# Moving the v projection of each second half into the first half's window, in a fused transformer block on one core

## The chip, the cores and the metric

The kernel runs on one core of a Trainium2 chip. The metric is the device time of one execution in microseconds (us), median of several runs. The engines are named as the profile names them: PE (TensorE matmuls), PEld (TensorE weight loads), DVE (VectorE), ACT (ScalarE), POOL (GpSimd) and SP (the queue that issues nearly all DMAs).

## What is computed

A transformer block with conditioned layer norms (D = 512 features, H = 16 heads of 32, hidden size 2048) over x of 8 sequences with 1024 tokens each, all in float32:

```python
mod = silu(condition) @ Wada + bada            # six vectors of 512 per sequence
sh_a, sc_a, gt_a, sh_m, sc_m, gt_m = split(mod, 6, axis=1)
xm = layernorm(x, g1, be1) * (1 + sc_a) + sh_a
q, k, v = heads(xm @ Wqkv)
x = x + gt_a * (softmax(causal(q @ k.T) * scale) @ v @ Wproj + bproj)
xm = layernorm(x, g2, be2) * (1 + sc_m) + sh_m
x = x + gt_m * (gelu(xm @ W1 + b1) @ W2 + b2)
```

## The kernel before

**Blocks and windows.** Each sequence is cut into two halves of 512 tokens, so there are 16 blocks n = 0 to 15; even n is a first half, odd n a second half. Through causality a first half attends to itself alone, a second half to both halves: it needs k and v of both. Window w is the stretch in which the attention of block w is issued. Beside it run the linear steps (projections and MLP) of neighbouring blocks, in an order written out by hand in a dictionary `plan[w]`, lines 236 to 269. Steps are `("k", n)`, `("q", n)`, `("v", n)` (projections of block n), `("proj", n)` (output projection), `("at", n)` and `("mt", n)` (transposes of the normalized rows, for attention and MLP), `("u", n, i)` (up projection, i = 0 to 3) and `("d", n, part)` (down projection, four parts). The MLP of block w - 1 begins in window w, and what is left over stands in `late` and opens window w + 1.

Before the change an odd window w opens with `late`, which holds ("u", w-2, 3), two parts of d, the transposes ("at", w+1), the other two parts of d; then comes ("v", w). An even window opens with two parts of d and ("v", w). Later in both come load_xr, proj (w-1), k (w+1), mt (w-1), q (w+1), and u of block w-1. Window 15 opens with one u, proj 14, mt 14 and four parts of d, then ("v", 15). Window 0 already holds ("v", 1); windows 0 and 1 are not touched.

**One projection** (`strassen`, line 773) is made with seven products of half size, each of four calls of `matmul`, and each of these four column-tiled TensorE instructions of 256 columns (line 205). The weights come as seven 256 KB pieces through a ring of nine tiles, loaded in the order of the plan by SP (`fetch`). Results leave the PSUM banks through DVE and ACT. Three PSUM banks (`ps_l`) serve all linear steps; four more form the one tile `st`/`sc` of the attention, one holds its output `po`.

**Attention.** A second half has 26 units of weights in its window, a first half 10. A unit is: scores `sc` (line 1476, row-tiled) and their maxima on DVE (line 1493) for the next group; then `weights_T`: `st` (lines 1557 and 1569, row-tiled), the exponential on ACT (line 1582), for diagonal units the mask on POOL (line 1587), sums of the weights on POOL (line 1695); then `weigh`: `po` (line 1610). TensorE works through one queue in the order in which the program was written; that order is chosen when the program is built, by a small model of each engine's clock. `step_aside` (line 1337) issues linear work ahead of an attention instruction until that instruction is ready by the model; `pace` adds to the linear work that is due, at a rate that spreads the linear work planned for a window over its attention:

```python
1720            stream["rate"] = planned_time(n) / mine * (0.7 if n == 0 else 1.0)
```

Where an attention step needs a result that is not made yet, the linear work is driven on until it is there, without any attention between. For v this stands in `close`, which issues the `po` of a unit:

```python
1333    def until(condition):
1334        while not condition():
1335            work()
1755        until(lambda: n - blocks[n][1] + parts[-1][0] // NTT in valued)
```

In a second half the first four units of a group use v of the first half, the others v of the second half; `valued` gets block n when its v is complete. `project_v` (line 882) may start once `free for v` of its block is set, which in the window of a first half happens at its first unit for both halves; `v` has two buffers. `("mt", n)` waits for `v done` of block n + 1 (line 1246), because it takes the buffer of the normalized input that v read.

The down projection (`down`, line 1073) subtracts halves of the hidden activations `hT` on DVE (line 1088) and through `either` (lines 162 and 165, which picks DVE or POOL by the model).

Of the kernel before, what the change touches and what calls it, by code (L numbers as in the profile page):

```python
# [22 lines left out]
def kernel(  # L23
# [66 lines left out]
    blocks = [(b, h) for b in range(B) for h in range(NHALF)]  # L90
# [140 lines left out]
    def mlp_steps(n):  # L231
        return [("u", n, i) for i in range(NQ)] + [("d", n, part) for part in range(4)]
# [8 lines left out]
    late = []  # L241
    for w in range(1, NB):
        n = w - 1
        m = mlp_steps(n)
        even = blocks[n][1] == 0
        rows_a = [("rows", blocks[n][0], "a")] if even else []
        rows_m = [("rows", blocks[n][0], "m")] if even else []
        own = m[:1] + ([("load_xa", w + 2)] if w + 2 < NB else []) + m[1:3]
        own += [("norm_a", w + 2)] if w + 2 < NB else []
        if w == NB - 1:  # L250
            steps = late[:1] + [("load_xr", n)] + rows_a + [("proj", n), ("mt", n)] + late[1:]
            steps += [("v", w)] + rows_m + own + m[3:6]
            late = m[6:]
        else:

            steps = late + [("v", w), ("load_xr", n)] + rows_a + [("proj", n), ("k", w + 1)]
            if w == 1:
                steps = [("load_xr", n)] + rows_a + [("k", w + 1), ("proj", n)]
            steps += [("mt", n), ("q", w + 1)] + rows_m + own
            at = [("at", w + 2)] if w + 2 < NB else []  # L260
            if blocks[w][1] == 0:

                late = m[3:6] + at + m[6:]
            else:
                steps += m[3:6] + at
                late = m[6:]
        plan[w] = steps
    n = NB - 1
# [1601 lines left out]
```

## Time and profile before

| what | value |
|---|---|
| median of 3 runs | 3526.36 us (3525.41 to 3528.59) |
| the profiled execution | 3526.6 us, span of its instructions 3524.9 us |
| granted TensorE clock, mean | 0.999 |
| DVE / ACT / POOL busy | 53% / 36% / 59% |
| LDWEIGHTS (PEld) busy | 51% |
| HBM traffic | 123 GB/s over the span |

The profile is one execution. Its busy time of an engine is the time in which at least one instruction of that engine ran; a wait's releaser is what ended the idle time. In the order of time, a row of the timeline is a run of equal instructions, with its start, its length and their count; in these rows a `matmul` call shows as eight PE records, so a projection is 224 of them.

### The profile page before, as it was taken

Reading aid. Unit: us, or ns where it says so; the run is one execution under the profiler, and the core shown is the slowest. Engines: PE = TensorE matmul, PEld = TensorE weight load, DVE = VectorE, ACT = ScalarE, POOL = GpSimd, SP = SyncE. Lnnn points to the kernel's source line nnn. Section 1 sums busy time; section 2 is a strip of 40 time slices with the busy share of each in tenths; the row PEclk is TensorE's granted clock in tenths of the full one; section 3 lists DMA queues with packets and bytes.
Section 4 is the critical chain, followed back from the end, with each engine's and each line's share of the span. In section 5 each row is a group of like instructions: output and inputs, shape, how many; then the busy total and the mean of one; then the engine's idle time right before and its main releaser. Section 6 shows DMA issues by size and latency. Waiting matters only on the chain.

```text
span 3524.9 us, 123741 instructions
## 1 busy us (share of the span) xinstructions
PE 3482.2 (99%) x56189; PEld 1800.1 (51%) x56189; DVE 1882.3 (53%) x2086; ACT 1286.5 (36%) x1422; POOL 2065.1 (59%) x2205
## 2 busy tenths in 40 slices
PE   7999999999999999999999999999999999999999
PEld 4444455445554554545545455454554545545445
DVE  5765664554635456364563645635446354554463
ACT  2335243352433514235152352514424244241521
POOL 3676755665456664576645766557664576644650
PEclk9999999999999999999999999999999999999999
DMA  6842334334343343533435334353343533434234
GB/s 208 267 143 89 115 109 120 123 106 142 107 139 103 109 142 103 155 100 100 145 99 159 97 103 139 101 157 99 104 139 100 156 101 108 131 100 151 89 118 137
DMA packets 319945, 441.76 MB, mean 125 GB/s; under 512 B 26569, under 2 KB 188677, under 8 KB 319421
## 3 DMA queue, kind: packets, MB, share of 16 engines
q1 hardware_dynamic: 319168, 433.54, 40.2%
q8 instruction: 443, 7.26, 0.8%
q14 instruction: 82, 0.66, 0.1%
q10 hardware_dynamic: 252, 0.29, 0.0%
HBM read 404.32 MB, written 29.41 MB: 123 GB/s over the span
## 4 chain that ended last, share of the span: by engine, by line
PE 93%; DVE 2%; POOL 2%; DMA 1%; issue 1%; ACT 1%; SPq 0%; DVEq 0%; POOLq 0%; ACTq 0%
PE bank L205 64%; PE sc L1476 9%; PE po L1610 7%; PE st L1569 7%; PE st L1557 2%; PE bank L656 2%; DVE mx L1493 2%; PE bank L1631 2%; POOL pT L1695 1%; PE bank L1531 0%; POOL hT L165 0%; DVE sc L1490 0%; DMA w<-in_L_cond_Wada_dram 0%; DMA hat<-in_x_dram 0%; DMA w<-in_L_cond_Wproj_dram 0%
## 5 line engine op out<-in xcount | busy, mean ns | idle before, releaser
L1695 POOL TENSOR_TENSOR pT<-pT,pT 128x256 f32<-128x256 f32 (+3 forms) x1254 | 1179.0, 975 | 202.0 <-ACT pT L1582 115.8
L1582 ACT ACTIVATE pT<-st 128x2048 f32<-128x2048 f32 x288 | 541.1, 1879 | 1046.0 <-PE st L1569 933.0
L205 PE MATMUL bank<-w,hT 128*32 128x256 f32 x14336 | 797.5, 379 | 0.1
L1493 DVE TENSOR_REDUCE mx<-sc 128x4 f32<-128x2048 f32 (+3 forms) x384 | 665.9, 1755 | 133.8 <-PE sc L1476 127.1
L205 PEld LDWEIGHTS bank<-w,hT 128*32 128x32 f32 x14336 | 451.9, 110 | 331.1 <-issue 26.6
L205 PE MATMUL bank<-xm_m,w 128*32 128x256 f32 x8192 | 499.4, 381 | 0.0
L205 PE MATMUL bank<-t_m,w 128*32 128x256 f32 x6144 | 383.9, 380 | 0.0
L205 PEld LDWEIGHTS bank<-xm_m,w 128*32 128x32 f32 x8192 | 252.1, 110 | 242.6 <-issue 80.9
L1587 POOL TENSOR_SCALAR_AFFINE_SELECT pT<-pT 128x512 f32<-128x512 f32 x256 | 165.2, 663 | 326.1 <-ACT pT L1582 324.6
L1476 PE MATMUL sc<-kT,qT 32*128 32x512 f32 (+3 forms) x3072 | 329.1, 520 | 5.7 <-DVE mx L1493 3.1
L1610 PE MATMUL po<-pT,v 128*32 128x512 f32 (+3 forms) x3072 | 305.6, 492 | 3.1 <-POOL pT L1587 3.1
L1490 DVE TENSOR_TENSOR sc<-sc,mask 128x1024 f32<-128x1024 f32 (+1 forms) x160 | 162.9, 1018 | 256.6 <-PE sc L1476 204.1
L1569 PE MATMUL st<-qT,kT 32*128 32x512 f32 (+3 forms) x3072 | 299.9, 486 | 0.0
L205 PEld LDWEIGHTS bank<-t_m,w 128*32 128x32 f32 x6144 | 192.1, 110 | 180.5 <-issue 52.7
L205 PE MATMUL bank<-xm_a,w 128*32 128x256 f32 x3968 | 250.3, 382 | 0.0
L197 DVE TENSOR_TENSOR hT<-bank,u_u 128x512 f32<-128x512 f32 x192 | 129.1, 686 | 158.1 <-PE bank L205 155.9
L165 POOL TENSOR_TENSOR qT<-top,rec 128x512 f32<-128x512 f32 x61 | 78.0, 1278 | 227.5 <-ACT rec L1649 227.5
L1476 PEld LDWEIGHTS sc<-kT,qT 32*128 32x128 f32 x3072 | 129.5, 183 | 155.1 <-ACT pT L1582 63.6
L205 PE MATMUL bank<-w,qT 128*32 128x256 f32 (+1 forms) x2944 | 191.0, 399 | 1.3 <-DMA w<-in_L_cond_Wproj_dram 1.3
L1030 ACT ACTIVATE hT<-hT,cols 128x512 f32<-128x512 f32 x256 | 164.2, 711 | 54.9 <-DVE hT L197 54.3
L205 PE MATMUL bank<-t_a,w 128*32 128x256 f32 x2944 | 183.9, 380 | 0.0
L205 PEld LDWEIGHTS bank<-xm_a,w 128*32 128x32 f32 x3968 | 122.9, 110 | 100.1 <-issue 17.6
(211 smaller groups left out, 3477.8 us busy)
## 6 DMA issues: line engine op xcount, KB each, us to landing
w<-in_L_cond_W_dram SPq DMA_DIRECT2D x384, 256.0 KB
w<-kept_up_S SPq DMA_DIRECT2D x256, 256.0 KB
w<-kept_down_S SPq DMA_DIRECT2D x256, 256.0 KB
w<-kept_qkv_S SPq DMA_DIRECT2D x180, 256.0 KB
w<-in_L_cond_Wqkv_dram SPq DMA_DIRECT2D x147, 256.0 KB
hat<-in_x_dram SPq DMA_DIRECT2D x64, 256.0 KB
xr<-in_x_dram SPq DMA_DIRECT2D x64, 256.0 KB
out_dram<-xr SPq DMA_DIRECT2D x64, 256.0 KB
```

The source lines that it names most:

```text
L165: nc.gpsimd.tensor_tensor(out, a, b, op)
L197: nc.vector.tensor_tensor(out, src, other, op)
L205: nc.tensor.matmul(ps[r, :], lhsT[:, r], rhs, start=start, stop=stop, skip_group_check=True)
L1030: nc.scalar.activation(hT[:, i, :], hT[:, i, :], AF.Gelu, bias=cols[:, O_B1 + f : O_B1 + f + 1])
L1476: nc.tensor.matmul(sc[:, j, c0 : c0 + w], qTs[n][r, gg, ts(qt, P)], keys_of(n, kh)[r, gg, :w], start=True, stop=True, skip_group_check=True,)
L1490: nc.vector.tensor_tensor(place, place, shape_of.to_broadcast(place.shape), ALU.add)
L1493: nc.vector.tensor_reduce(maxima[n, gg][:, kh, qt, :], sc[:, :, c0 : c0 + w], axis=AX.X, op=ALU.max)
L1569: nc.tensor.matmul(st[:, j, c0 : c0 + w], kT[r, gg, ts(k % NTT, P)], qT[r, gg, TB - w :], start=False, stop=True, skip_group_check=True,)
L1582: nc.scalar.activation(pT[:, :, :used], st[:, :, :used], AF.Exp, scale=scale)
L1587: nc.gpsimd.affine_select(diagonal, diagonal, pattern=[[0, HPG], [1, P]], compare_op=ALU.is_ge, fill=0.0, base=0, channel_multiplier=-1,)
L1610: nc.tensor.matmul(po[r, TB - w :], v[:, k % NTT, g * P + j * hd : g * P + (j + 1) * hd], pT[:, j, c0 : c0 + w], start=(k == 0), stop=last ...
L1695: nc.gpsimd.tensor_tensor(into, into, pT[:, j, c0 : c0 + w], ALU.add)
```

## The change

The v projection of block w, for odd w from 3 to 15, is taken out of window w (in windows 3 to 13 from behind `late`, in window 15 from behind the parts of d) and put into window w - 1, behind ("q", w) and ahead of the u steps that follow there. First halves keep theirs at the front of their own window. The guards, the buffers, the number of steps and the arithmetic are the same; the order in which SP loads the weight pieces follows the plan.

```diff
@@ -249,14 +249,14 @@
         if w == NB - 1:
             steps = late[:1] + [("load_xr", n)] + rows_a + [("proj", n), ("mt", n)] + late[1:]
-            steps += [("v", w)] + rows_m + own + m[3:6]
+            steps += rows_m + own + m[3:6]
             late = m[6:]
         else:
-            steps = late + [("v", w), ("load_xr", n)] + rows_a + [("proj", n), ("k", w + 1)]
+            steps = late + ([] if even else [("v", w)]) + [("load_xr", n)] + rows_a + [("proj", n), ("k", w + 1)]
             if w == 1:
                 steps = [("load_xr", n)] + rows_a + [("k", w + 1), ("proj", n)]
-            steps += [("mt", n), ("q", w + 1)] + rows_m + own
+            steps += [("mt", n), ("q", w + 1)] + ([("v", w + 1)] if blocks[w][1] == 0 else []) + rows_m + own
```

In this loop n is w - 1 and `even` is true when block n is a first half, that is, when w is odd.

## The prediction

> **What bounds the kernel now.** I read the page's busy times and chain first, then TensorE's busy time in three stretches (windows 0 and 1, windows 2 to 14, window 15 and the end), then its list of waits in the middle one.
>
> ```profile
> span 3524.9 us, 123741 instructions
> PE 3482.2 (99%) x56189; PEld 1800.1 (51%) x56189; DVE 1882.3 (53%) x2086; ACT 1286.5 (36%) x1422; POOL 2065.1 (59%) x2205
> PEclk9999999999999999999999999999999999999999
> PE 93%; DVE 2%; POOL 2%; DMA 1%; issue 1%; ACT 1%; SPq 0%; DVEq 0%; POOLq 0%; ACTq 0%
> ```
>
> ```profile
> 0.00:399.00 399.00, 372.18 (x6037) 1.00 0.52 166
> 399.00:3128.30 2729.30, 2724.08 (x43975) 1.00 0.40 120
> 3128.30:3525.00 396.70, 385.99 (x6188) 0.99 0.40 121
> ```
>
> ```profile
> engine line waited for: us in total, times, longest us
> PE bank L1531 <- POOL mcols L1515: 2.5, 4, 0.7
> PE sc L1476 <- DVE mx L1493: 1.6, 7, 0.5
> ```
>
> TensorE is never short of work. Six of the seven moves lie between 399 and 3128 us, and there it idles 2729.30 - 2724.08 = 5.2 us in all; its named waits there are 2.5 and 1.6 us. The other idle time is the start (399.00 - 372.18 = 26.8 us, before anything that changes) and window 15 with the end (396.70 - 385.99 = 10.7 us). The clock is granted in full. A move of work can thus take away only these few us, or add new idle time; what DVE, ACT and POOL gain or lose beneath costs nothing until TensorE waits.
>
> **What the move touches.** This is TensorE's timeline in window 11, at the place where v is made now.
>
> ```profile
> 2287.21 0.61 PE L205 MATMUL bank<-t_m,w 128*32 128x256 f32 x8
> 2287.64 1.91 PE L205 MATMUL bank<-xm_m,w 128*32 128x256 f32 x32
> 2289.37 0.61 PE L205 MATMUL bank<-t_m,w 128*32 128x256 f32 x8
> 2289.91 1.15 PE L1476 MATMUL sc<-kT,qT 32*128 32x384 f32 x16
> 2290.99 1.50 PE L205 MATMUL bank<-t_m,w 128*32 128x256 f32 x24
> ...
> 2298.08 0.41 PE L1531 MATMUL bank<-ident_b,mcols 128*32 128x128 bf16 x16 [0.74 <-POOL mcols L1515]
> 2298.31 24.35 PE L205 MATMUL bank<-w,hT 128*32 128x256 f32 x448
> 2322.59 2.18 PE L656 MATMUL bank<-ident,hat 128*128 128x128 f32 x16
> 2324.78 20.93 PE L205 MATMUL bank<-w,hT 128*32 128x256 f32 x384
> 2345.53 1.91 PE L205 MATMUL bank<-w,xm_a 128*32 128x256 f32 x32
> ...
> 2357.62 1.48 PE L205 MATMUL bank<-w,qT 128*32 128x256 f32 x24
> 2358.91 1.04 PE L1610 MATMUL po<-pT,v 128*32 128x512 f32 x8
> ```
>
> From 2298 to 2358 no attention instruction is issued: the fifth unit's `po` needs v of the second half, so `close` drives the linear work through the rest of d (24.3 us), `at` (2.2), d again (20.8) and v, 2345.53 to 2357.62 = 12.1 us. Only then does `po` follow. With v made a window earlier this forced stretch has no reason left: d and `at` will be spread by `pace` among the odd window's 26 units. The even window gets 12.1 us more linear work and keeps its own forced stretch, for its own v.
>
> **The sum.**
>
> *The work itself.* 7 projections x 12.1 us = 84.6 us change windows and none vanish. Is a matmul dearer between attention instructions? In the forced stretch 448 records take 2322.59 - 2298.31 = 24.28 us, 54.2 ns each. Between attention instructions the 32 records at 2287.64 take 1.73 us until the next row, 54.1 ns each. The eight at 2289.37 take 0.54 us instead of 0.43: entering the row-tiled scores costs 0.11 us. But scores and `st` stand in the same PSUM tile and never follow each other directly, and the kernel has as many of them after as before; the number of these entries is fixed. Term: 0.
>
> The Trainium skill (Perfetto Trace Analysis, Identifying the Most-Contended Engine) says that matmul busy time does not measure how near TensorE is to its limit, and that the busy share of weight loads does; by that, 51% would leave headroom for a better mix to use. The equal 54 ns in both kinds of stretch contradict it here: the 99% is a full queue at an unchanged rate.
>
> *Evacuation.* Each v takes eight sums and copies from PSUM with it, to an even window that must have room.
>
> ```profile
> L197 DVE TENSOR_TENSOR v<-bank,u_v x48: 680/692/692, 68.5 to 3235.1; 128x512 f32<-128x512 f32 x48
> L192 ACT COPY v<-bank x15: 586/586/587, 60.8 to 3228.2; 128x512 f32<-128x512 f32 x15
> ```
>
> ```profile
> core 0: us, PE busy (x) PEld busy (x) DVE busy (x) ACT busy (x) POOL busy (x), PEclk, DMA share, GB/s
> 2088.20:2261.50 173.30, 172.98 (x2896) 93.81 (x2893) 93.33 (x101) 55.01 (x67) 92.42 (x112) 1.00 0.42 127
> 2261.50:2297.80 36.30, 35.84 (x528) 16.48 (x524) 20.82 (x27) 21.55 (x23) 24.29 (x22) 1.00 0.28 85
> 2297.80:2356.20 58.40, 58.11 (x1064) 34.31 (x1068) 15.95 (x20) 10.72 (x15) 29.68 (x24) 1.00 0.52 162
> 2356.20:2521.40 165.20, 165.20 (x2508) 79.33 (x2500) 94.23 (x106) 74.56 (x75) 114.44 (x122) 1.00 0.35 106
> ```
>
> The first row is window 10, the others are window 11 before, in and behind the forced stretch. Eight of 0.69 us are 5.5 us; DVE is busy 93.33 of 173.30 us in the even window and becomes (93.33 + 5.5) / (173.30 + 12.1) = 53%, the same share. Hidden under TensorE; with that cover gone it would cost 5.5 us per window. Term: 0.
>
> *Loads.* SP issues the seven pieces of each v earlier, in the plan's new order, ahead of those of u instead of behind those of d; nothing else is queued past them except x rows and the gate rows, whose places in the plan stay. The forced stretch draws pieces at the highest rate (162 GB/s, DMA share 0.52) and TensorE does not wait for one; spreading lowers that. Term: 0.
>
> *A wait that goes.* The 0.74 us ahead of the forced stretch is the maxima of the next group passing POOL; nearly all of the four such waits (2.5 us in all) stand there. Spread linear work can cover them. Between -2.5 and 0; I take -2.
>
> *Transposes for the MLP.* In the odd window `mt` is cut into pieces, each of which costs TensorE two changes of shape.
>
> ```profile
> 2411.10 0.33 PE L656 MATMUL bank<-ident,xh_m 128*128 128x128 f32 x1
> 2411.36 0.64 PE L205 MATMUL bank<-xm_a,w 128*32 128x256 f32 x8
> 2411.93 0.33 PE L656 MATMUL bank<-ident,xh_m 128*128 128x128 f32 x1
> ```
>
> A single transpose takes 0.26 us to the next row and makes the eight matmuls behind it last 0.57 instead of 0.43, while one of the sixteen at 2322.59 takes 2.19 / 16 = 0.14: a cut costs about 0.26 us. How many there are depends on when ACT delivers the rows. Two cuts fewer or more in seven windows are 7 x 2 x 0.26 = 3.6 us either way; `at`, whole today, could be cut likewise. I take 0.
>
> *The d parts beside attention.* This is the part that can hurt. They put long subtractions of `hT` on POOL, ahead of the attention's masks. Today they mostly run in forced stretches. One place shows them meeting, near the end (POOL first, then TensorE).
>
> ```profile
> 3378.29 5.58 POOL L165 TENSOR_TENSOR hT<-hT 128x1024 f32<-128x1024 f32 x2
> 3383.83 0.63 POOL L1587 TENSOR_SCALAR_AFFINE_SELECT pT<-pT 128x512 f32<-128x512 f32 x1
> ```
>
> ```profile
> 3384.51 1.07 PE L1610 MATMUL po<-pT,v 128*32 128x512 f32 x8 [2.47 <-POOL pT L1587]
> ...
> 3393.59 8.82 PE L205 MATMUL bank<-w,hT 128*32 128x256 f32 x160
> 3402.22 1.04 PE L205 MATMUL bank<-w,qT 128*32 128x512 f32 x8
> ```
>
> TensorE idled 2.47 us: `po` waits for the mask, which is queued behind 5.58 us of `hT`, and everything behind `po` on TensorE waits with it. The odd windows already end with u and two parts of d beside attention, and the list of waits from 399 to 3128 us has no entry of this kind. So six stretches paid 0 and one paid 2.47. The bounds for the seven moved stretches, with two pairs of such subtractions each, are 0 and 7 x 2 x 2.47 = 34.6 us. I take one meeting, +2.5, nearer to the many zeros.
>
> *Window 15.* Attention ends near 3393 us; the last 8.6 us of d (3393.59 to 3402.22) then cover the chain from the last sums to the final projection. If the spread order used that d up earlier, up to 8.6 us would lie bare; if it removed the 2.47 us, that much would be won. Same steps, same pacing rule: I take 0, bounds -2.5 and +8.6.
>
> Sum: -2 + 2.5 = +0.5 us on 3526.6 us (the profiled execution, span 3524.9 and 1.7 around it), which is 0.2 above the median of 3526.36. Forecast: 3527 us, no change within what a measurement of this kernel can tell, 0.2% or 7 us.
>
> **The rivals.** *Slower: POOL's queue.* With no forced stretch, d's subtractions meet masks and sums in every odd window. For it: the 2.47 us wait, and POOL's share of 114.44 / 165.20 = 69% behind the forced stretch against 51% in it. Against it: the six odd windows that end this way unharmed. If half of the 14 meetings cost 2.47 us it adds 17 us: 3543 us; all of them, 3561. It decides the sign from four meetings on (3 x 2.47 = 7.4 us), that is, where the linear work put ahead of `po` is shorter than POOL's backlog by the actual times.
>
> *Faster: mixing the two regimes pays.* The forced stretch leaves ACT at 10.72 / 58.40 = 18% and POOL at 51%, the rest loads them with 45% and 69%; evened out, every wait might go. All that TensorE can get back is 5.2 us in the middle, 2.5 in window 15, and up to 3.6 of cuts: -11 us, 3515 us. It needs most of them together. The Trainium skill (Perfetto Trace Analysis, Optimization Strategy) recommends interleaving regimes whose most-contended engine differs; here TensorE is the most contended in both, so the rule's condition fails.
>
> *It does not do what it says.* If another need held the linear work (k and q of the next block, the transposes), a forced stretch would remain in some window with the same sum: 3526 us.
>
> **How the numbers follow.** Forecast 0.52; slower through POOL or a bare end 0.28; faster 0.16; the move without effect 0.04. Same is the first and last, 0.56. For 8 in 10 the range takes -8 us (half of the faster cases) and +16 us (most of the slower ones, nearly to seven meetings): 3518 to 3543. The cases of "same" alone lie at 3520 to 3533.
>
> **What would show it.** Right: in odd windows no run of linear rows over 30 us is left, the v rows stand behind q in even windows, TensorE's busy time stays at 3482 within 4 us, and windows 2 to 14 idle 3 to 8 us. A POOL theory would show as TensorE waits for `pT` L1587 or L1695 in the odd windows; cuts as more rows of L656. The prediction is wrong if TensorE's busy time itself moves by over 7 us, for then the number or the price of its shape changes is not fixed as I argue, or if idle time grows where I named nothing.

## The result: 1.3% slower, and the profile after

| kernel | median | against before (95% interval) |
|---|---|---|
| before | 3527.5 us (4 runs) | |
| changed | 3574.5 us (4 runs, 3568.7 to 3577.0) | 1.0133 (1.0121 to 1.0145) |

The forecast was 3527 us, at most 3543. The loss is 47 us. The page of the changed kernel, the same lines as before, and TensorE's busy time in the same three stretches (windows 0 and 1, 2 to 14, 15 and the end):

```profile
span 3573.0 us, 123722 instructions
PE 3497.5 (98%) x56189; PEld 1810.3 (51%) x56189; DVE 1915.6 (54%) x2108; ACT 1296.8 (36%) x1437; POOL 2046.3 (57%) x2168
PE 90%; POOL 4%; DVE 2%; DMA 2%; issue 1%; ACT 1%; SPq 0%; DVEq 0%; POOLq 0%; ACTq 0%
```

```profile
0.00:399.00 399.00, 373.40 (x6037) 0.99 0.51 166
399.00:3178.50 2779.50, 2737.35 (x43976) 0.99 0.38 118
3178.50:3573.00 394.50, 386.75 (x6188) 0.99 0.39 121
```

In the middle TensorE now idles 2779.50 - 2737.35 = 42.2 us, where it idled 5.2. And it is busy for 3497.5 us in all instead of 3482.2, with the same 56189 instructions. Over the whole span idle time went from 42.7 to 75.5 us (+32.8) and busy time up by 15.3 us: together the 48.1 us by which the span grew. The list of TensorE's waits in the middle stretch names the new ones; its columns are who waited for whom, us in total, times, longest.

```profile
PE bank L205 <- DVE u_proj L197: 19.4, 4, 7.5
PE bank L205 <- DVE y L197: 8.1, 2, 4.3
PE bank L1631 <- DVE y L197: 5.5, 1, 5.5
PE st L1557 <- DVE mx L1493: 4.3, 5, 1.9
PE bank L1531 <- POOL mcols L1515: 2.7, 2, 1.8
```

The first three lines are seven waits, 33.0 us in all: one of 3.8 to 7.5 us in each odd window from 3 to 13, and a second of 1.0 us in window 13. TensorE has no free PSUM bank, because DVE doesn't empty one. The view of the gate row's tile says what DVE waits for (idle time of the engine that uses it, by releaser), and SP's own list of waits what stands before that.

```profile
  DMA row_ga<-kept_ga: 47.3, 6
```

```profile
SPq L1230 <- DMA out_dram<-xr: 16.6, 7, 4.3
```

Neither entry exists before the change. The timeline of window 5 shows one of the six long waits, cause first:

```profile
1098.04 1.65 SPq L1070 DMA_DIRECT2D out_dram<-xr  x2
1101.53 1.76 SPq L1230 DMA_DIRECT2D xr<-in_x_dram  x4
1103.34 0.43 SPq L506 DMA_DIRECT2D row_ga<-kept_ga  x1
...
1108.95 0.69 DVE L197 TENSOR_TENSOR y<-bank,row_ga 128x512 f32<-128x512 f32 x1 [8.80 <-DMA row_ga<-kept_ga]
1109.56 0.68 DVE L197 TENSOR_TENSOR u_proj<-bank,u_proj 128x512 f32<-128x512 f32 x1
...
1110.29 1.08 PE L205 MATMUL bank<-w,qT 128*32 128x256 f32 x8 [7.46 <-DVE u_proj L197]
1111.15 1.94 PE L1610 MATMUL po<-pT,v 128*32 128x512 f32 x8
```

The residual `xr` has one buffer. The last d part stores it; the x rows of the next block are loaded into it; behind them come the gate rows of the new sequence (`rows_a`, in odd windows alone); then the output projection starts, and its second evacuation multiplies by `row_ga`. SP issues in order: the store at 1098.0 us; then it stands until the store has landed; at 1101.5 the four x rows; at 1103.3 the gate row, which lands at 1108.9. DVE has waited for it for 8.8 us, with everything behind it in its queue. Before the change v stood ahead of these loads. In window 11 of that kernel:

```profile
2349.22 1.96 SPq L1070 DMA_DIRECT2D out_dram<-xr  x2
...
2354.89 1.83 SPq L1230 DMA_DIRECT2D xr<-in_x_dram  x4
2356.77 0.57 SPq L506 DMA_DIRECT2D row_ga<-kept_ga  x1
...
2368.68 0.68 DVE L197 TENSOR_TENSOR y<-bank,row_ga 128x512 f32<-128x512 f32 x1
```

There 5.7 us lie between the store and the x rows, in which SP issues weight pieces while v runs (2345.53 to 2357.62 us), and SP's list names no wait for that store. The output projection begins at 2357.62, after the gate row was issued, and DVE uses the row 11.9 us behind its issue, without a wait.

The second part of the loss is the clock. Stretches of the changed kernel (length, TensorE's busy time, granted clock) at the second and third of these waits, where the clock was halved:

```profile
1107.60:1114.40 6.80, 4.11 (x24) 0.50 0.61 230
1551.40:1558.20 6.80, 4.74 (x44) 0.50 0.79 234
```

Each of the six long waits is followed, or still accompanied, by 6.83 us at half clock: in the timeline above the same `po` of 512 columns lasts 1.94 us at 1111 and 1.07 elsewhere. In these six stretches TensorE is busy for 27.6 us together. Half of that, 13.8 us, is about what its busy time in the middle stretch grew by (2737.35 - 2724.08 = 13.3); the other 2.0 of the 15.3 us lie in the first and last stretch.

The Trainium skill (TensorE: Matmul & The Clock Gate, HAM oscillation — how this bites in real kernels) says that a TensorE idle for over about 3.4 us falls back to half clock. The six idle times of 3.8 to 7.5 us agree with that, but shorter ones had the same effect. In the kernel before, the 2.47 us wait for the mask had none, while a wait of 2.70 us at 3417.3 us had (length, TensorE's busy time, granted clock):

```profile
3417.40:3420.80 3.40, 0.40 (x2) 1.00 0.35 117
3420.80:3424.20 3.40, 3.40 (x21) 0.50 0.03 5
```

In one of the kernels below (the loads ahead of v) a wait of 2.47 us had it too, so here the measurement decides. The clock records of all nine traces show more. The half clock begins only at points of a grid of 3.41 us and lasts one, two or three steps of it: 3.41, 6.83 or 10.24 us (leaving out the last one of each trace, which reaches past the kernel's end). Behind the first 390 us, a step at full clock with over 2.0 us of idle time was always followed by half clock, one with under 1.2 us never; between the two it went both ways. So it matters less how long a wait is than how much of one step it fills.

### The profile page after: what moved, and what is told of

Read it like the earlier page. It is cut to its first block, busy times and chain, and to the rows that moved or that the text cites. A ratio compares the mean times of both kernels' runs of the same rounds, so it can differ in the third digit from the quotient of the medians.

```text
span 3573.0 us, 123722 instructions
## 1 busy us (share of the span) xinstructions
PE 3497.5 (98%) x56189; PEld 1810.3 (51%) x56189; DVE 1915.6 (54%) x2108; ACT 1296.8 (36%) x1437; POOL 2046.3 (57%) x2168
## 4 chain that ended last, share of the span: by engine, by line
PE 90%; POOL 4%; DVE 2%; DMA 2%; issue 1%; ACT 1%; SPq 0%; DVEq 0%; POOLq 0%; ACTq 0%
PE bank L205 62%; PE sc L1476 8%; PE po L1610 7%; PE st L1569 6%; PE st L1557 2%; POOL pT L1695 2%; PE bank L656 2%; PE bank L1631 2%; DMA row_ga<-kept_ga 1%; DVE mx L1493 1%; PE bank L1531 0%; DMA out_dram<-xr 0%; POOL xr L165 0%; DVE sc L1490 0%; ACT pT L1582 0%
## 5 line engine op out<-in xcount | busy, mean ns | idle before, releaser
L1695 POOL TENSOR_TENSOR pT<-pT,pT 128x256 f32<-128x256 f32 (+3 forms) x1254 | 1213.6, 1003 | 227.0 <-PE po L1610 112.7
L205 PE MATMUL bank<-w,hT 128*32 128x256 f32 x14336 | 810.6, 380 | 0.1
```

What stands on the lines that cost most here:

```text
L205: nc.tensor.matmul(ps[r, :], lhsT[:, r], rhs, start=start, stop=stop, skip_group_check=True)
L1695: nc.gpsimd.tensor_tensor(into, into, pT[:, j, c0 : c0 + w], ALU.add)
```

## The experiments

Theory Q: the gate row comes late, because SP stands at the store, as v no longer lies between. Theory P is the prediction's slower rival, POOL's backlog through d beside attention. Theory E: the even windows, with one v more, are overfull. Each ratio is against the kernel before on the same chip: 3527.2 us for the first four kernels, 3528.2 for the other three.

**The gate rows ahead of the x rows.**

```diff
-            steps = late + ([] if even else [("v", w)]) + [("load_xr", n)] + rows_a + [("proj", n), ("k", w + 1)]
+            steps = late + ([] if even else [("v", w)]) + rows_a + [("load_xr", n)] + [("proj", n), ("k", w + 1)]
```

> The changed kernel with the two gate-row loads issued ahead of the four x-row loads instead of behind them (same place in the plan, same work). Theory Q (SP's queue): in the odd windows the x-row load waits for the store of the same buffer to land, the gate row queues behind it and lands 5 to 6 us too late, DVE holds the PSUM banks, TensorE idles 4 to 7 us six times and then runs 6.8 us at half clock. With the rows ahead of that wait they land some 5 us sooner (one store landing, four issues and four larger transfers less): most of the idle time goes, 3530 to 3545 us, granted clock back to 0.998 or more. Theory P (POOL's backlog from the d subtractions beside attention): nothing changes, 3570 to 3577 us. Theory E (the even windows are overfull): nothing changes, 3570 to 3577 us.

3538.5 us, 1.0029 (1.0018 to 1.0041). Swapping two neighbouring steps in SP's queue gave back 36 of 47 us. DVE's waits for the row shrank:

```profile
  DMA row_ga<-kept_ga: 8.7, 4
```

The row still queues behind the store's issue, which waits for POOL's last addition to `xr`. The next kernel takes it out from behind that too.

**The gate rows at the front of the odd window.**

```diff
-            steps = late + ([] if even else [("v", w)]) + [("load_xr", n)] + rows_a + [("proj", n), ("k", w + 1)]
+            steps = rows_a + late + ([] if even else [("v", w)]) + [("load_xr", n)] + [("proj", n), ("k", w + 1)]
```

> The changed kernel with the two gate-row loads issued at the very front of each odd window, ahead of the d parts left over; the x-row load stays where it is. Theory Q: the row has landed tens of us before its use, so the six waits of 4 to 7 us and the half clock behind them are gone: 3520 to 3532 us. If instead the x rows themselves (which still wait for the store) hold things up, POOL and DVE wait for them in place of the gate row and the time stays above 3545 us. Theories P and E: 3570 to 3577 us.

3527.6 us, 1.0002 (0.9993 to 1.0011): the whole loss is gone, with all seven v where the change put them. Theories P and E fall. SP still stands at the store for the x rows, and POOL now waits for them, seven times:

```profile
POOL xr L165 <- DMA xr<-in_x_dram: 21.4, 7, 5.9
```

But none of TensorE's waits comes of that. The kernel's page, the stretch of windows 2 to 14 and TensorE's longest waits there:

```profile
span 3526.7 us, 123719 instructions
```

```profile
399.00:3132.20 2733.20, 2722.95 (x43976) 1.00 0.39 120
```

```profile
PE st L1557 <- DVE mx L1493: 4.7, 6, 1.9
PE bank L1531 <- POOL mcols L1515: 2.7, 2, 1.8
```

TensorE idles 10.2 us there, and no wait names a mask on POOL.

**k ahead of the output projection.**

```diff
-            ... + rows_a + [("proj", n), ("k", w + 1)]
+            ... + rows_a + ([("k", w + 1), ("proj", n)] if even else [("proj", n), ("k", w + 1)])
```

> The changed kernel with the k projection of the next block ahead of the output projection in the odd windows (as window 1 has it), the loads staying in front of both. Theory Q: the 12 us of k cover the store, the x rows and the gate row just as v did before: 3520 to 3535 us, no wait for the gate row. Theories P and E: the same work stands beside the same attention, 3565 to 3580 us.

3539.4 us, 1.0038 (1.0024 to 1.0052); slower than expected, though the wait for the gate row is gone. k had been the cover of something else: the transposes `mt` follow the output projection directly now and wait for ACT's normalized rows. The list of the middle stretch:

```profile
PE bank L656 <- ACT xh_m L594: 7.4, 20, 0.7
PE st L1557 <- DVE mx L1493: 5.8, 6, 2.8
```

So a cover taken from one step uncovers the next: TensorE idles 17.5 us in the middle stretch of this kernel, against 10.2 with early gate rows. The wait of 2.8 us (for DVE's maxima) was followed by half clock too (length, TensorE's busy time, granted clock):

```profile
2883.90:2894.10 10.20, 9.07 (x68) 0.50 0.00 0
```

About half of these 9.07 us is the clock's, again behind a wait of under 3.4 us.

**v moved within its own window only.** From the kernel before:

```diff
-            steps = late + [("v", w), ("load_xr", n)] + rows_a + [("proj", n), ("k", w + 1)]
+            steps = late + ([("load_xr", n)] + rows_a + [("proj", n), ("v", w)] if even else [("v", w), ("load_xr", n), ("proj", n)]) + [("k", w + 1)]
```

> The kernel before with the v of the odd windows 3 to 13 moved only behind the output projection of its own window: no even window gets anything, and d stays in a forced stretch without attention. Theory Q: the cover between the store and the output projection is gone all the same, so the gate row is late in six windows: 3555 to 3580 us with waits of DVE for the gate row. Theory P: d still runs without attention beside it, so 3522 to 3533 us. Theory E: the even windows are as before, 3522 to 3533 us.

3579.3 us, 1.0149 (1.0131 to 1.0168). No even window got anything, d ran in its forced stretch without attention, and the whole loss is there. DVE's waits for the row:

```profile
  DMA row_ga<-kept_ga: 60.4, 6
```

And the timeline in window 3, the same picture as in the changed kernel:

```profile
626.10 0.69 DVE L197 TENSOR_TENSOR y<-bank,row_ga 128x512 f32<-128x512 f32 x1 [10.40 <-DMA row_ga<-kept_ga]
...
626.92 1.27 POOL L165 TENSOR_TENSOR xr<-xr,y 128x512 f32<-128x512 f32 x1 [8.93 <-DVE y L197]
...
627.44 1.08 PE L205 MATMUL bank<-w,qT 128*32 128x256 f32 x8 [7.39 <-DVE u_proj L197]
```

DVE, POOL and TensorE all stand for the one row.

**The gate rows issued by ACT.** From the changed kernel, in `gate_broadcasts`:

```diff
-            nc.sync.dma_start(row, kept_rows[name][b : b + 1, :].to_broadcast([P, D]))
+            nc.scalar.dma_start(row, kept_rows[name][b : b + 1, :].to_broadcast([P, D]))
```

> The changed kernel, every load of a gate row issued by ACT instead of SP, at the same place in the plan behind the x-row load. Theory Q1 (the gate row is late because SP issues in order and stands at the x-row load until the store has landed): ACT passes that wait, the row is issued some 4 to 6 us sooner, 3525 to 3535 us. Theory Q2 (it is late because the DMA engines are full of x rows and weight pieces then): the row still shares the engines with them, 3550 us or more.

3531.5 us, 1.0010 (1.0000 to 1.0019), with no wait for the row left. Q1 holds: the row was late through its place in SP's queue, not through the DMA engines' load. The Trainium skill (DMA: Bandwidth & Descriptors, Issuing engines are not separate DMA queues) says that issuing from several engines only saves the usually small time of the sequencer. Here 24 loads of gate rows moved to another issuer saved 43 us, because the first issuer stood at another transfer's wait; the measurement decides.

**The loads ahead of v.** From the kernel before:

```diff
-            steps = late + [("v", w), ("load_xr", n)] + rows_a + [("proj", n), ("k", w + 1)]
+            steps = late + ([("load_xr", n)] + rows_a + [("v", w)] if even else [("v", w), ("load_xr", n)]) + [("proj", n), ("k", w + 1)]
```

> The kernel before with only the x-row and gate-row loads of the odd windows ahead of v instead of behind it (v stays in its odd window, ahead of the output projection). SP now stands at the store's landing as in the changed kernel. Theory Q: that alone costs nothing, since v's 12 us still lie between it and the output projection: 3522 to 3532 us. If SP's stall also starves the weight loads, TensorE waits for pieces of w: 3540 us or more.

3539.3 us, 1.0035 (1.0020 to 1.0050); outside what Q gave, at the edge of the other. No wait for the gate row remains, as v covers it. But SP standing at the store (13.8 us in all) delays the weight pieces queued behind it:

```profile
PE bank L205 <- DMA w<-kept_proj_S: 3.8, 4, 1.3
PE bank L1531 <- DVE xm_m L660: 2.8, 6, 0.5
```

With the named waits TensorE idles 13.4 us in windows 2 to 14 of this kernel instead of 5.2. So SP's stand has a price of its own, which the place of v before the loads avoided too. Another 1.7 us go to 3.41 us at half clock behind the 2.47 us wait for the mask in window 15; the kernel before has that wait without the half clock. How the rest of the 11 us divides is open.

**Block 15's v alone.** From the kernel before:

```diff
-            steps += [("v", w)] + rows_m + own + m[3:6]
+            steps += rows_m + own + m[3:6]
...
-            steps += [("mt", n), ("q", w + 1)] + rows_m + own
+            steps += [("mt", n), ("q", w + 1)] + ([("v", w + 1)] if w + 1 == NB - 1 else []) + rows_m + own
```

> The kernel before with only the v of block 15 moved to window 14; the other six stay. In window 15 the output projection already stood ahead of v, so nothing loses its cover. Theory Q: no wait for the gate row; the 2.5 us wait for the mask near the end may go as in the other kernels with this move: 3523 to 3527 us. If moving a v by itself costs what a seventh of the loss is, 3534 us.

3524.4 us, 0.9988 (0.9979 to 0.9997). In window 15 the output projection already stood ahead of v, so no cover was lost; from 3130 us on the list of TensorE's waits has one line:

```profile
PE bank L656 <- ACT xh_m L623: 3.5, 3, 2.7
```

The 2.47 us wait for the mask is gone. Of the seven moves this one alone is a small gain, and with it the fastest of the kernels, by 0.12%; the interval only just leaves out no change.

## Why the prediction was wrong

*Loads, the step that failed.* It put them at 0 because the x rows' and gate rows' places in the plan stay. Their places stayed, but what stood ahead of them was the very step that moved. The question asked was what v's own pieces are queued past; the one to ask was what v had been covering: a store, four loads and the gate row, in one in-order queue, up to the output projection. Measured: 33.0 us of waits, and 13.8 us lost to half clock behind them, a consequence that stood in no term. I read the wait for data in the kernel before, found none, and took it for a proof that there is slack.

*The work itself* (0): right. With the gate rows early, TensorE is busy for 3481.5 us against 3482.2 before, with v moved and the forced stretches gone (in the odd windows from 3 on they were 55.6 to 70.9 us long; with the change no stretch without attention there is over 16 us). So the price of a matmul didn't depend on the mix here.

*Evacuation* (0): right; v in an even window cost nothing with the gate rows early, and the loss is there without any v in an even window (v moved within its own window).

*A wait that goes* (-2): wrong in size and sign. With the gate rows early, windows 2 to 14 idle 10.2 us, not 3 to 8: the wait for the maxima stays at 2.7 us, in two places instead of four, and `st` waits 4.7 us for DVE's maxima, which were hidden before.

*Transposes* (0): no measurable share.

*The d parts beside attention* (+2.5) and *window 15* (0, bound -2.5): there was no wait for a mask in the odd windows, and the one near the end went. Together these two were about 5 us too dear, and the wait that was to go was about 7 us too cheap. That the sum of 0.5 us fits the kernel with early gate rows (3527.6) is thus in part luck, errors that cancel; it does not fit the one that was forecast.

*The rivals.* The slower one had the right sign and the wrong mechanism: where d runs without attention and v still stands behind the output projection, the loss is full. The faster one, mixing regimes, is answered by the kernel with early gate rows: all the mixing, and 1.0002. The move did what it says, so the third falls too. Of the prediction's own tests, idle time that grows where nothing was named came true. So did the other one, TensorE's busy time moving by over 7 us (15.3), but not for the reason given there: with early gate rows it is 3481.5 us again, so it was the clock and not the number or the price of the shape changes.

## What to carry to other kernels

Before moving a step away, ask what follows it and whether its operands are on their way while it runs; a trace without a wait shows that the cover suffices, not that none is needed. Loads that an in-order queue issues behind one that must wait for its buffer are late with it: issue what is ready and needed soon ahead of it, or from another engine. Where TensorE is full, moving work gains nothing but can open gaps, and gaps cost again through the clock: those of 3.8 to 7.5 us always did here, those of 2.5 to 2.8 us mostly.

## What the hardware showed unexpectedly

The half clock goes by steps of 3.41 us. It lasted two of them, 6.83 us, at each of the six waits, whether the idle time was 3.8 or 7.5 us, and so added two fifths to their price (13.8 on 33.0 us). And the delay of one broadcast row of 256 KB stopped three engines: DVE at the multiplication, TensorE through the full PSUM banks, and POOL behind DVE's result.
